# Attention and graph layer on one core: order of the parts of a step, and the softmax denominators over 32 columns with one reciprocal spread through DRAM

## The chip, the cores and the metric

The kernel runs on one core of one Trainium2 chip. The metric is the device time of one execution in microseconds (us). The kernel before takes 3855.4 us in the median of ten runs, 3853.72 to 3857.78.

## What is computed

Thirty-two samples of 512 tokens with 512 features go through two layers with the same 512 x 512 adjacency matrix. Layer 0 is attention with eight heads of 64 features under a mask, layer 1 a graph attention whose logits are a sum of two numbers per token pair. All is float32.

```python
def _L0_gnn_ref(x, adj, Wq, bq, Wk, bk, Wv, bv, Wo, bo):
    q, k, v = (x @ Wq + bq), (x @ Wk + bk), (x @ Wv + bv)     # each reshaped to (b, n, 8, 64)
    scores = jnp.einsum('bqhd,bkhd->bhqk', q, k) / jnp.sqrt(jnp.float32(HD))
    scores = scores + (1.0 - adj)[None, None, :, :] * -1000000000.0
    attn = jax.nn.softmax(scores, axis=-1)
    out = jnp.einsum('bhqk,bkhd->bqhd', attn, v).reshape(b, n, d)
    return out @ Wo + bo
def _L1_gnn_ref(x, W, a, beta, mask):
    h = jnp.einsum('bnc,cf->bnf', x, W)
    s1, s2 = h @ a[:F_, 0], h @ a[F_:, 0]
    e = leaky_relu(s1[:, :, None] + s2[:, None, :], 0.2) * mask[None, :, :]
    att = jax.nn.softmax(e, axis=2)
    return jax.nn.elu(jnp.einsum('bij,bjf->bif', att, h) + beta * h)

h = jnp.maximum(_layernorm(x), 0.0);  x = x + L0(h, adj)
h = jnp.maximum(_layernorm(x), 0.0);  x = x + L1(h, adj)
```

## The kernel before

**Products.** A 512 x 512 x 512 product is done with seven products of half size instead of eight (`seven`, line 428). Its pieces come in a fixed order: A11 with b11 into PSUM bank x, S1 with t1 into bank qz[0], S2 with t2 onto y (which ScalarE has filled with a copy of x), A12 with b21 onto x, S3 with t3 onto z = qz[1] (filled with a copy of y), S4 with b22 onto y, NA22 with t4 onto z. So the third piece waits for the copy y<-x, the fifth for the copy z<-y. The sums t1 to t4 of the right operand are made by GpSimd (POOL): `combos`, `first_combo`, `other_combos`, `fourth`. Five such products are done for each sample: v, q, k, Wo (names with _w) and the final one with W (names with _y).

**Attention.** The eight heads go in four pairs j. A *unit* (b, j) does the values of the pair before it, po<-e,v (`values`, into bank po, 16 matmul instructions of 512 columns), and then the scores of its own pair in four blocks k of 128 keys: ps<-qT,kT into the banks s, then x and y, then qz, then s again (`scores`). VectorE adds the mask to each block (e, lines 562 and 567), ScalarE takes the exponential (line 582), VectorE adds the four blocks up to es (line 579). `denominators(b, j)`, the "." in the order of a step, calls `finish` for the pair before: a product of ones with es gives pd, the denominators, each repeated on 64 partitions (line 620), VectorE takes the reciprocal in two halves of 256 columns (line 628), ScalarE copies rd onto itself to get its sum for the later check of range (line 633), and POOL multiplies the unnormalised output oT with it (line 634).

**Other parts of a step.** V, W, K, Q: the products v, Wo, k, q. D: the diagonal and the denominators of layer 1. G: gather, the four products pg<-at,hn of layer 1 (13.7 us), whose results ScalarE copies to gT. X: the three sums of POOL over gT. Y: the final product with W, followed for each quarter by the ELU: ScalarE exponential (line 811), VectorE lines 814 and 816 (and 836 ahead of them for two of the four quarters), POOL adds x1 (line 824), SP stores. N: transposes of the normalised next sample through banks po, qz and s (`turn`), with ReLU on ScalarE. H: POOL's sums over hT. U: POOL's sums over oT. r, R: loads of x for the residual, and the addition of c_row.

**Order.** TensorE, VectorE, ScalarE and POOL run their instructions in the order in which the program emits them. The parts of a step are given by a string, for most samples

```python
}.get(b, "0.VDU1.GX2.rYNRWH3.KQ")
```

in which a digit is a unit of sample b, V and Q belong to samples b and b+1, Wo to b-1, and D, G, X, Y to b-2. Work of VectorE that has slack is not emitted at once, but given to a planner (`later`, `then`, line 186) with an earliest time, a due time and a cost. It is emitted when the planner's own clocks of TensorE and VectorE (`pe(us)`, `dve(us)`) say that it fits; `need(key)` emits all that is left of a kind. The list GAP (line 44) sets due times for the sums es and for the reciprocals.

Of the kernel before, what the change touches and what calls it, by code (L numbers as in the profile page):

```python
# [9 lines left out]
F32 = mybir.dt.float32  # L10
# [3 lines left out]
AF = mybir.ActivationFunctionType  # L14
ALU = mybir.AluOpType
# [6 lines left out]
P = 128  # L22
HD = 64
# [13 lines left out]
H = 256  # L37
# [3 lines left out]

A11, A12, NA22, S1, S2, S3, S4 = range(7)

GAP = (12.0, 14.0, 28.0, 24.0)
GAPS = {0: (14.0, 1.0, 4.0, 24.0), 1: (12.0, 12.0, 2.0, 14.0)}
LAST_GAPS = (3.0, 14.0, 12.0, 3.0)

# [16 lines left out]
def kernel(  # L64
# [23 lines left out]
    nc = tc.nc  # L88
    B, N, D = x.shape
    T = N // P  # L90
    C = D // P
    NP = D // P
# [58 lines left out]
    def wtile(shape, name, tag, bufs, dt=F32):  # L151
        return work.tile(shape, dt, name=name, tag=tag, bufs=bufs)
# [12 lines left out]
    def pe(us):  # L165

        clock["pe"] += us
        till = clock["pe"] + (1.0 if at_ends[0] else 0.4)
        while True:
            due = [i for i, (_, t, _) in enumerate(ends) if t <= till]  # L170
            fits = [
                (by, i) for i, (_, t, cost, _, by) in enumerate(spare)
                if max(clock["dve"], t) + cost <= till
            ]
            if due:
                ends.pop(due[0])[2]()
            elif fits:
                run_spare(min(fits)[1])
            else:
                return  # L180
# [5 lines left out]
    def later(key, wait, by, cost, fn):  # L186

        now = max(clock["dve"], clock["pe"])
        spare.append((key, now + wait, cost, fn, now + by))

    def then(key, fn, wait=0.0):

        ends.append((key, clock["dve"] + wait, fn))
# [202 lines left out]
    def fourth(b, name, B):  # L396

        B["t4"] = wtile([P, 2, H], f"{name}4_{b}", "T", 5)
        nc.gpsimd.tensor_tensor(B["t4"], B["t2"], B["b21"], op=ALU.subtract)

    def turn(b, st):

        xs = st["x"]
        need(("x", b))
        h = [pair(b, "hT", i, "hP", 2) for i in range(2)]

        def turned(p, c):
            for t in range(T):
                nc.tensor.transpose(p[:, ts(t, P)], xs[t][:, ts(c, P)], ident)  # L409

        def second():
            for c, tag in ((2, "po"), (3, "qz")):
                p = psum.tile([P, 1 if c == 2 else 2, N], F32, name=f"pn{c}_{b}", tag=tag)[:, 0, :]
                turned(p, c)
                nc.scalar.activation(h[1][:, c - 2, :], p, AF.Relu)

        def first():
            p = psum.tile([P, 2, N], F32, name=f"pn0_{b}", tag="s")
            for c in range(2):
                turned(p[:, c, :], c)  # L420
            nc.scalar.activation(h[0], p, AF.Relu)

        for part in (second, first) if b else (first, second):
            part()
        pe(2.4)
        st["h"] = h

# [115 lines left out]
    def gap(b, j):  # L543
        return (LAST_GAPS if b == B - 1 else GAPS.get(b, GAP))[j]

# [69 lines left out]
    def finish(b, j, st):  # L615

        need("rd")
        pd = psum.tile([P, N], F32, name=f"pd_{b}_{j}", tag="pd")
        for s in range(2):
            nc.tensor.matmul(  # L620
                pd[s * HD : (s + 1) * HD, :], ones[:, :HD], st["es"][j][:, s, :], start=True, stop=True
            )
        pe(0.95)
        o = st["o"][j // 2][:, j % 2, :]
        rd = wtile([P, N], f"rd_{b}_{j}", "rd", 1)

        def divide(k):
            nc.vector.reciprocal(rd[:, ts(k, H)], pd[:, ts(k, H)])  # L628
            if k:
                then("rd", rest)  # L630

        def rest():
            nc.scalar.activation(rd, rd, AF.Copy, accum_out=rsum[:, b, j : j + 1])  # L633
            nc.gpsimd.tensor_tensor(o, o, rd, op=ALU.mult)  # L634

        finished.add((b, j))
        release()
        for k in range(2):
            later("rd", 0.0, gap(b, (j + 1) % NP) + 3.0, 1.7, lambda k=k: divide(k))

    def residual(b, st, i, tag="x1", bufs=3):

# [18 lines left out]
    def out_proj(b, st):  # L661
        x1 = st["x1"]
        st["mv"] = wtile([P, T, 2], f"mv1_{b}", "mv1", 2)
        st["s12"] = wtile([P, 2, T], f"s12_{b}", "s12", 2)
        st["hn"] = [None] * T

        def parts(k, i, p):

            n = 2 // len(x1[k])
            for u, r in enumerate(x1[k]):  # L670
                yield r[:, :, ts(i, H)], quarter(p)[:, u * n : (u + 1) * n, :]

        def add(i, k, p):
            for r, p_ in parts(k, i, p):
                nc.vector.scalar_tensor_tensor(r, p_, 1.0 / VS, r, op0=ALU.mult, op1=ALU.add)  # L675
                dve(0.75 if len(x1[k]) == 1 else 0.45)

        def one(i, k, p):
            add(i, k, p)
            if i == 1:  # L680
                norm1(b, st, (0, 1))

        def two(i, k, p, r):
            add(i, k, p)
            if i == 0:
                norm1(b, st, (2, 3))

        def more(q_):
            for i in (1, 0):
                for r, q in parts(1, i, q_):  # L690
                    nc.gpsimd.tensor_tensor(r, r, q, op=ALU.add)

        return seven(f"w{b}", wo, st["oT"], True, one, two, 1.0 / VS, more)
# [173 lines left out]
    def step(b):  # L867

        cur, nxt = states.get(b), states.get(b + 1)
        prev, old = states.get(b - 1), states.get(b - 2)

        def run(pieces):
            for _ in pieces:
                pass

        def V():
            run(proj_v(b, cur))

        def G(cs=range(C)):
            for c in cs:
                gather(b - 2, c, old)

        def y_(g):
            st = states[g]
            st["pieces"] = final(g, st)
            for _ in range(3):
                next(st["pieces"])

            B = st["gB"]
            B["t4"] = B["t2"]
            nc.gpsimd.tensor_tensor(B["t4"], B["t2"], B["b21"], op=ALU.subtract)

        def z_(g):
            run(states[g]["pieces"])

        def Y():
            y_(b - 2)
            z_(b - 2)  # L900

        def X():
            old["gB"] = combos(b - 2, "vT", old["g"])

        def G1():

            G((0, 1))
            t1 = first_combo(b - 2, "vT", old["g"][0], nc.gpsimd)
            G((2, 3))
            old["gB"] = other_combos(b - 2, "vT", old["g"], t1)  # L910

        def turned():
            turn(b + 1, nxt)
            if b + 2 < B:
                new_state(b + 2)

        def W():
            need("wa")
            fourth(b - 1, "uT", prev["oT"])
            run(out_proj(b - 1, prev))  # L920


        def H_():
            nxt["hT"] = combos(b + 1, "tT", nxt["h"])

        def K():
            fourth(b + 1, "tT", nxt["hT"])
            run(proj_k(b + 1, nxt))

        def U():  # L930
            need("rd")
            if b == B:
                prev["oT"] = other_combos(b - 1, "uT", prev["o"], prev["t1"])
            else:
                prev["oT"] = combos(b - 1, "uT", prev["o"])

        def T1():
            cur["t1"] = first_combo(b, "uT", cur["o"][0], nc.gpsimd)

        parts = {  # L940
            "V": V, "D": lambda: diagonal(b - 2, old), "G": G, "Y": Y, "N": turned, "W": W,
            "y": lambda: y_(b - 3), "z": lambda: z_(b - 3), "X": X, "g": G1,
            "K": K, "U": U, "H": H_, "r": lambda: residual(b - 1, prev, 0, *(("e", 4) if b == B else ())),
            "t": T1, "n": lambda: run_all(("hn", b - 1)), "J": judge,
            "R": lambda: residual(b - 1, prev, 1, *{B: ("e", 4), B - 1: ("x", 4)}.get(b, ())),
            "Q": lambda: run(proj_q(b + 1, nxt)),
            "c": lambda: value_row(ao, bvr), "w": row_constants,
        }
        order = {
            0: "0.V1.NH2c.3wK.Q", 1: "0.VUrR1.W2.NH3K.Q", B - 1: "0.VDU1.rRGX2.W3.t", B: "0yrR.zUWDngY",  # L950
            B + 1: "DgJY",
        }.get(b, "0.VDU1.GX2.rYNRWH3.KQ")
        unit_ = 0
        at_ends[0] = b < 2 or b >= B - 1
        for part in order:
            if part.isdigit():
                unit_ = int(part)
                unit(b, unit_)
            elif part == ".":
                denominators(b, unit_)  # L960
            else:
                parts[part]()
        states.pop(b - 3, None)
# [260 lines left out]
```

## Time and profile before

| | us |
|---|---|
| median of ten runs | 3855.4 |
| the profiled execution, its own time | 3855.6 |
| its span, first to last instruction | 3853.8 |
| TensorE busy | 3623.1 |
| VectorE busy | 2829.1 |
| ScalarE busy | 1478.0 |
| POOL busy | 1291.6 |
| TensorE's waits behind the transposes, line 409 | 160.0 |
| mean granted TensorE clock | 0.971 of full |

A group of the profile gives line, engine, operation, out<-in, shape and count, then busy time and mean ns of one, then the idle time of the engine just before it and what ended it. A line of waits gives who waited for whom, the total in us, how often, and the longest. A line of a timeline gives start and length in us, engine, line, operation, tiles, shape and count, and in brackets the idle time before it. Matmuls are pipelined: the time that one costs is the distance to the next start, not its length. The chip's DMA traffic is low, 31 GB/s in the mean.

### The profile page before, as it was taken

To read this page: it belongs to the slowest core of one execution; us is meant where nothing else is said; L and a number is where in the kernel's file an instruction comes from. 1 tells how busy PE (TensorE), PEld (TensorE's weight loads), DVE (VectorE), ACT (ScalarE), POOL (GpSimd) and SP (SyncE) were. 2 spreads that over 40 slices of the span, in tenths; PEclk is the share of its full clock that TensorE was granted. 3 is DMA by queue.
4 is the path that set the end of the run, shared out by engine and by line. 5 is a ranking of instruction groups with operands and counts; after the bars stand their busy time and mean duration, and the time that the engine had idled before them with its cause. 6 is when DMAs were issued, how large, how long until landed. Compare 5 with 4: busy or idle time off the path is not lost. (4 is left out here: it accounts for less than half of the span.)

```text
span 3853.8 us, 62639 instructions
## 1 busy us (share of the span) xinstructions
PE 3623.1 (94%) x25846; PEld 2024.3 (53%) x25846; DVE 2829.1 (73%) x4335; ACT 1478.0 (38%) x2310; POOL 1291.6 (34%) x1090
## 2 busy tenths in 40 slices
PE   9999999999999999999999999999999999999986
PEld 5555555555554555555555545555455555555543
DVE  7978767787677777677877778767777777787674
ACT  3433333343433433343434334333433333343332
POOL 5432333322333232333223332334332233322341
PEclk9999999999999999999999999999999999999998
DMA  3010111001110001111011110111110111101100
GB/s 124 17 37 4 37 36 36 34 6 34 37 36 34 20 20 37 36 34 36 4 37 36 36 34 9 31 37 36 34 35 6 36 37 36 34 4 37 31 25 26
DMA packets 88035, 120.82 MB, mean 31 GB/s; under 512 B 11904, under 2 KB 49792, under 8 KB 87744
## 3 DMA queue, kind: packets, MB, share of 16 engines
q1 hardware_dynamic: 86160, 114.91, 9.3%
q8 instruction: 205, 3.36, 0.4%
q10 hardware_dynamic: 1376, 1.57, 0.1%
q14 instruction: 86, 0.70, 0.1%
q0 software_dynamic: 208, 0.27, 0.0%
HBM read 83.11 MB, written 33.62 MB: 30 GB/s over the span
## 5 line engine op out<-in xcount | busy, mean ns | idle before, releaser
L634 POOL TENSOR_TENSOR oT<-oT,rd 128x512 f32<-128x512 f32 x128 | 170.5, 1332 | 1624.2 <-ACT rd L633 1624.2
L582 ACT ACTIVATE e<-e 128x1024 f32<-128x1024 f32 x512 | 541.1, 1057 | 191.7 <-DVE e L567 157.6
L567 DVE SCALAR_TENSOR_TENSOR e<-maskT,ps 128x1024 f32<-128x1024 uint8 x384 | 454.3, 1210 | 145.2 <-PE ps L555 145.0
L555 PE MATMUL ps<-qT,kT 64*128 64x512 f32 x2048 | 483.3, 605 | 12.4 <-DVE e L567 12.4
L605 PE MATMUL po<-e,v 128*64 128x512 f32 x2048 | 462.9, 592 | 0.0
L53 PE MATMUL pg<-at,hn 128*64 128x512 f32 x2048 | 449.1, 597 | 4.2 <-DVE dmax L788 2.1
L628 DVE RECIPROCAL rd<-pd 128x256 f32<-128x256 f32 x256 | 434.8, 1728 | 1.2 <-POOL oT L634 1.2
L579 DVE TENSOR_TENSOR es<-es,e 128x1024 f32<-128x1024 f32 x254 | 342.0, 1347 | 16.9 <-ACT e L582 1.1
L555 PEld LDWEIGHTS ps<-qT,kT 64*128 64x128 f32 x2048 | 183.9, 186 | 309.3 <-issue 214.0
L53 PEld LDWEIGHTS pg<-at,hn 128*64 128x64 f32 x2048 | 148.5, 138 | 298.3 <-issue 290.0
L605 PEld LDWEIGHTS po<-e,v 128*64 128x64 f32 x2048 | 156.6, 138 | 236.3 <-issue 226.4
L409 PE MATMUL pn<-ident,x 128*128 128x128 f32 x512 | 106.4, 378 | 160.4 <-DVE y L816 160.0
L824 POOL TENSOR_TENSOR y<-y,x 128x512 f32<-128x512 f32 x124 | 157.3, 1269 | 243.1 <-DVE y L816 202.6
L613 ACT COPY oT<-po 128x512 f32<-128x512 f32 x128 | 73.9, 577 | 397.5 <-PE po L605 397.5
L675 DVE SCALAR_TENSOR_TENSOR x<-x_w,x 128x512 f32<-128x512 f32 x32 | 22.0, 689 | 273.0 <-issue 261.5
L729 DVE CUSTOM_DVE_ANT_0 scr<-hn,wa_r 128x512 f32<-128x512 f32 x256 | 167.9, 711 | 49.0 <-ACT hn L716 49.0
L756 ACT ACTIVATE at<-at 128x512 f32<-128x512 f32 x128 | 80.4, 628 | 274.8 <-DVE at L752 274.8
L633 ACT ACTIVATE rd<-rd 128x512 f32<-128x512 f32 x128 | 80.7, 630 | 272.4 <-DVE rd L628 272.3
L334 POOL TENSOR_TENSOR rs<-rs,mhalf 128x2 f32<-128x2 f32 (+1 forms) x97 | 77.9, 804 | 318.5 <-DVE rs L333 314.8
L409 PEld LDWEIGHTS pn<-ident,x 128*128 128x128 f32 x512 | 87.5, 198 | 179.9 <-issue 179.1
L654 POOL TENSOR_TENSOR x<-x,c_row 128x512 f32<-128x512 f32 x124 | 158.5, 1300 | 49.1 <-DMA x<-in_x_dram 49.1
L814 DVE TENSOR_SCALAR y<-y 128x512 f32<-128x512 f32 x128 | 61.5, 480 | 152.0 <-ACT y L811 152.0
(221 smaller groups left out, 6794.5 us busy)
## 6 DMA issues: line engine op xcount, KB each, us to landing
x<-in_x_dram SPq DMA_DIRECT2D x128, 256.0 KB, 4.5
out_dram<-y SPq DMA_DIRECT2D x128, 256.0 KB, 2.1
x<-in_x_dram SPq DMA_DIRECT2D x63, 512.0 KB, 3.9
s<-row_s SPq DMA_DIRECT2D x32, 256.0 KB, 3.9
adj<-in_adj_dram SPq DMA_DIRECT2D x4, 256.0 KB, 7.6
wk<-in_L_gnn_Wk_dram ACTq DMA_DIRECT2D x3, 256.0 KB, 9.0
wq<-in_L_gnn_Wq_dram SPq DMA_DIRECT2D x3, 256.0 KB, 6.7
wv<-in_L_gnn_Wv_dram SPq DMA_DIRECT2D x3, 256.0 KB, 5.4
```

Of the source, the lines that this page charges most:

```text
L53: nc.tensor.matmul(out[s : s + HD], lhsT[:, s : s + HD], rhs, start=start, stop=stop, skip_group_check=onto)
L409: nc.tensor.transpose(p[:, ts(t, P)], xs[t][:, ts(c, P)], ident)
L555: nc.tensor.matmul(ps[s], st["kT"][j][rows, ts(k, P)], st["qT"][j][rows, :], start=True, stop=True)
L567: nc.vector.scalar_tensor_tensor(e, maskT[:, k, :].unsqueeze(1).to_broadcast([P, 2, N]), NEG, p, op0=ALU.mult, op1=ALU.add)
L579: (nc.gpsimd if early else nc.vector).tensor_tensor(es, one, e, op=ALU.add)
L582: nc.scalar.activation(e, e, AF.Exp)
L605: nc.tensor.matmul(po[s * HD : (s + 1) * HD, :], v[k // 2][:, k % 2, (2 * j + s) * HD : (2 * j + s + 1) * HD], e[k][:, s, :], start=k == 0 ...
L628: nc.vector.reciprocal(rd[:, ts(k, H)], pd[:, ts(k, H)])
L634: nc.gpsimd.tensor_tensor(o, o, rd, op=ALU.mult)
L654: eng.tensor_tensor(r[:, t, :], r[:, t, :], c_row, op=ALU.add)
L729: nc.vector.tensor_tensor_reduce(scr, st["hn"][t], r, 1.0, 0.0, op0=ALU.mult, op1=ALU.add, accum_out=st["s12"][:, g, t : t + 1],)
L824: (nc.vector if b == B - 2 else nc.gpsimd).tensor_tensor(yu, yu, x_[:, :, ts(i, H)], op=ALU.add)
```

## The change

**Order of a step.** For samples 2 to 30 the final product now comes directly behind its gather (g is the gather with POOL's sums among it), then a unit, then Wo and the transposes, then a unit, then k and q. M is W with the sum t4 emitted after three pieces of the product. The transposes use bank s first, then po and qz, in all samples. GAP has new values.

**Denominators.** The product of ones with es uses 32 columns of ones, four times for 256 columns of es, so that pd has (head, half of the queries) on four groups of 32 partitions and 256 columns. One reciprocal of 256 columns follows. ScalarE's copy for the sum goes to pd. One row of each group, 4 x 256 numbers, is written to DRAM by ScalarE's queue, and SP's queue reads it back twice, broadcast on 64 partitions each, into rd of 128 x 512. POOL's multiplication is as before; the planner emits it 6.0 us of its clock later.

```diff
-GAP = (12.0, 14.0, 28.0, 24.0)
+GAP = (13.0, 26.0, 14.0, 24.0)
...
-        for part in (second, first) if b else (first, second):
-            part()
+        first()
+        second()
...
-        pd = psum.tile([P, N], F32, name=f"pd_{b}_{j}", tag="pd")
+        pd = psum.tile([P, N], F32, name=f"pd_{b}_{j}", tag="pd")[:, :H]
         for s in range(2):
-            nc.tensor.matmul(
-                pd[s * HD : (s + 1) * HD, :], ones[:, :HD], st["es"][j][:, s, :], start=True, stop=True
-            )
-        pe(0.95)
+            for k in range(2):
+                r = (2 * s + k) * 32
+                nc.tensor.matmul(
+                    pd[r : r + 32, :], ones[:, :32], st["es"][j][:, s, ts(k, H)], start=True, stop=True
+                )
+        pe(0.55)
         o = st["o"][j // 2][:, j % 2, :]
         rd = wtile([P, N], f"rd_{b}_{j}", "rd", 1)
-        def divide(k):
-            nc.vector.reciprocal(rd[:, ts(k, H)], pd[:, ts(k, H)])
-            if k:
-                then("rd", rest)
-        def rest():
-            nc.scalar.activation(rd, rd, AF.Copy, accum_out=rsum[:, b, j : j + 1])
-            nc.gpsimd.tensor_tensor(o, o, rd, op=ALU.mult)
+        rq = rd[:, :H]
+        def divide():
+            nc.vector.reciprocal(rq, pd)
+            then("rd", spread)
+        def spread():
+            d = dram.tile([2, N], F32, name=f"rd_{b}_{j}", tag="rd")
+            nc.scalar.activation(pd, rq, AF.Copy, accum_out=rsum[:, b, j : j + 1])
+            nc.scalar.dma_start(d.rearrange("s (k q) -> (s k) q", k=2), rq[0:P:32, :])
+            for s in range(2):
+                nc.sync.dma_start(rd[s * HD : (s + 1) * HD, :], d[s : s + 1, :].to_broadcast([HD, N]))
+            then("rd", lambda: nc.gpsimd.tensor_tensor(o, o, rd, op=ALU.mult), 6.0)
         finished.add((b, j))
         release()
-        for k in range(2):
-            later("rd", 0.0, gap(b, (j + 1) % NP) + 3.0, 1.7, lambda k=k: divide(k))
+        later("rd", 0.0, gap(b, (j + 1) % NP) + 3.0, 1.7, divide)
...
+        def M():
+            pieces = out_proj(b - 1, prev)
+            for _ in range(3):
+                next(pieces)
+            fourth(b - 1, "uT", prev["oT"])
+            run(pieces)
...
-        }.get(b, "0.VDU1.GX2.rYNRWH3.KQ")
+        }.get(b, "0.VDU1.rgY2.RMNH3.KQ")
```

More of the change, by code (lines that the diff above doesn't have):

```diff
@@ L941, in step @@
             "V": V, "D": lambda: diagonal(b - 2, old), "G": G, "Y": Y, "N": turned, "W": W,
-            "y": lambda: y_(b - 3), "z": lambda: z_(b - 3), "X": X, "g": G1,
+            "y": lambda: y_(b - 3), "z": lambda: z_(b - 3), "X": X, "M": M, "g": G1,
             "K": K, "U": U, "H": H_, "r": lambda: residual(b - 1, prev, 0, *(("e", 4) if b == B else ())),
```

## The prediction, made before the changed kernel had run

> **What bounds the kernel now.** I read busy times first, then TensorE's waits, then the timelines of one steady step (samples 2 to 30 run one order, 29 times).
>
> ```profile
> PE 3623.1 (94%) x25846; PEld 2024.3 (53%) x25846; DVE 2829.1 (73%) x4335; ACT 1478.0 (38%) x2310; POOL 1291.6 (34%) x1090
> ...
> L628 DVE RECIPROCAL rd<-pd 128x256 f32<-128x256 f32 x256 | 434.8, 1728 | 1.2 <-POOL oT L634 1.2
> ```
>
> TensorE is busy nearly always, so work taken from VectorE counts only where TensorE waits for VectorE. TensorE's waits:
>
> ```profile
> PE pn L409 <- DVE y L816: 160.0, 29, 5.8
> PE pe L53 <- DVE as L763: 19.1, 2, 11.7
> PE ps L555 <- DVE e L567: 12.4, 33, 1.7
> ```
>
> One place, 29 times, 5.51 us each: the transposes behind the final product. The step that I use, TensorE first, then VectorE:
>
> ```profile
> 1810.32 1.90 PE L53 MATMUL qz_y<-w,vT 128*64 128x256 f32 x16
> 1812.14 0.66 PE L409 MATMUL pn<-ident,x 128*128 128x128 f32 x4
> 1818.31 2.79 PE L409 MATMUL pn<-ident,x 128*128 128x128 f32 x12 [5.50 <-DVE y L816]
> 1821.03 2.95 PE L53 MATMUL x_w<-wo,oT 128*64 128x256 f32 x16
> 1823.82 1.89 PE L53 MATMUL qz_w<-wo,oT 128*64 128x256 f32 x16
> ...
> 1834.18 3.60 PE L605 MATMUL po<-e,v 128*64 128x512 f32 x16
> 1837.71 3.70 PE L555 MATMUL ps<-qT,kT 64*128 64x512 f32 x16
> 1841.34 1.08 PE L620 MATMUL pd<-es,ones 128*64 128x512 f32 x4
> 1842.25 1.90 PE L53 MATMUL x_k<-hT,wk 128*64 128x256 f32 x16
> ```
>
> ```profile
> 1814.62 0.88 DVE L816 SCALAR_TENSOR_TENSOR y<-yq,rd,y 128x256 f32<-128x256 f32 x2
> 1816.55 0.63 DVE L814 TENSOR_SCALAR y<-y 128x512 f32<-128x512 f32 x1 [1.04 <-ACT y L811]
> 1817.29 0.88 DVE L816 SCALAR_TENSOR_TENSOR y<-qz_y,rd,y 128x256 f32<-128x256 f32 x2
> ```
>
> The last ELU of the final product reads qz until 1818.17, and the second transpose bank is qz. After the idle the clock is halved: in the stretches 1801 to 1819 and 1819 to 1835 the granted clock is 0.92 and 0.87, later 1.00. Twelve transposes take 2.72 us, against 0.109 each at full clock (sample 1, at 173.87), and the first product piece takes 2.79 against 1.73. Loss: 1.41 + 1.06 = 2.47 here. This step is 118.47 us long and the mean over 28 steps (wait ends 280.19 to 3593.20) is 118.32, so 2.3 on average.
>
> **The change, part by part** (us per steady step; SP's and POOL's new queue orders were read from the changed program).
>
> *Removed:* stall 5.51, half clock 2.3, and a 0.33 wait in unit 1 (scores for VectorE, late by two reciprocals of 3.36 at 1890.15; one of 1.73 ends in time). Sum 8.14. Without its stalls the step is about 110.
>
> *Denominators.* pd to the next product takes 0.91 now (1841.34 to 1842.25): 0.43 streaming for each of two passes, some 0.05 fill. The trace has no 32-column product. Lower end: four at once on half the columns, 0.91 - 0.43 = 0.48. Upper end: two at a time, 0.91 plus one more change of tile shape, 0.1 (the last scores' pass starts at 1840.82 and streams 0.43; pd starts at 1841.34, 0.1 late) = 1.0. The nearest row is the 16 small products of pe, 0.98 at 1886.92: 61 ns each, eight make 0.49, plus 0.1: I take 0.6. Gain 0.3 in units 1 to 3, 0.9; unit 0 below. The Trainium skill, "TensorEngine Tiling (Array Packing)", Key Properties, speaks against the edit: a change of tiling mode drains the array, while different tiles run in parallel. The trace agrees with the drain (that 0.1); by the page alone, without the 61 ns, one would write 0.43 + 0.1 and gain 0.4 a unit.
>
> *One reciprocal.* VectorE loses 1.73 four times a step. That is worth nothing further: it is off the path, except where a queue waits for it, next.
>
> *Unit 0: a new stall.* ScalarE's queue now has, of unit 0, three exponentials, the copy of rd, its DMA, the fourth exponential, then y_v<-x_v, without which v's third piece cannot start. The copy waits for the reciprocal behind the four mask additions:
>
> ```profile
> 1872.60 1.28 DVE L562 SCALAR_TENSOR_TENSOR e<-maskT,ps 128x512 f32<-128x512 uint8 x2
> 1873.80 2.34 DVE L567 SCALAR_TENSOR_TENSOR e<-maskT,ps 128x1024 f32<-128x1024 uint8 x2
> ```
> ```profile
> 1872.72 4.51 ACT L582 ACTIVATE e<-e 128x1024 f32<-128x1024 f32 x4 [0.97 <-DVE e L567]
> 1877.14 0.58 ACT L450 COPY y_v<-x_v 128x512 f32<-128x512 f32 x1
> ```
>
> Reciprocal 1876.06 to 1877.81; ScalarE starts 0.09 later (1893.51 to 1893.60 elsewhere); copy of 256 columns 0.4 (0.63 for 512); DMA issue 0.4 (0.37 to 0.52 on ACT's queue at the start; zero if it overlaps the copy); exponential 0.97; y_v copy 0.58; 0.07 to TensorE: 1880.32. The third piece of v starts at 1878.29 now: +2.03, from +1.6 to +2.4. A quicker pd gains nothing in this unit. Behind the late copy stand only q5_v and z of the same product, which are then early enough.
>
> *Final product directly behind its gather.* y's third piece needs vT2, 3.45 after the gather's end. POOL has ahead of it rd of unit 0's pair, which now waits for DRAM. From the gather's start g: sums es end at g + 5.6, reciprocal g + 7.35, ScalarE's copy behind the second gather copy g + 8.1, write 1.4 from issue (row_s<-s, 2 KB), two reads on SP 0.35 apart, 3.9 (s<-row_s, 256 KB in one; the stores of 256 KB take 2.1, x loads 4.5), so g + 14.2, a round trip of 6.1 with the waits between; POOL multiply 1.4, vT2 1.3: g + 16.9. TensorE asks at g + 13.73 + 3.45 = g + 17.2. Hidden, by the gather, with 0.3 to spare; beyond that every microsecond more of DMA costs one. POOL's power for the next sample's norm stands behind vT3, and two rows of VectorE wait for it ahead of the ELU: they end 7.1 after the product's start, the ELU is asked for at 8.0 (1807.95 now), so 0.9 to spare.
>
> ```profile
> s<-row_s SPq DMA_DIRECT2D x32, 256.0 KB, 3.9
> row_s<-s SPq DMA_DIRECT2D x32, 2.0 KB, 1.4
> ```
>
> *A unit behind the final product.* The ELU chain is unchanged: qz free 18.3 after the product's start (1799.96 to 1818.31). The unit's third scores now ask for it at 12.09 + 5.35 (po to third scores in the step shown) = 17.44: stall 0.9. VectorE adds the mask to the first scores only after the ELU, 1.2, so the fourth scores (bank s) wait 0.25 more. Sum 1.15. Next late: Wo's y copy behind the four exponentials, 0.15.
>
> *Transposes behind Wo, then a unit.* qz is free after one addition of 0.69, hidden by twelve transposes. But po, asked for next by the unit's values, is free only after ScalarE's ReLUs of the first two banks (1.02) and of po (0.6): about 2.75 after the start, against 1.9 of transposes. +0.85. The turned order (s, po, qz) puts it there.
>
> *Moved on other queues.* SP's x loads (4 x 0.4) now stand ahead of the reads of unit 2's rd; that rd holds POOL before tT4, which k needs 7 us later. The s1 row is read 1.4 + 3.9 + 0.3 behind the last dot, while VectorE has four kT rows (1.8) and three sums (3.7) and waits for hidden parts of k: some 1.4 to spare; beyond it VectorE is late for q's first bank. The out stores come behind reads that have landed before the final product's first ELU. Costed at nothing. The new GAP values only move positions in these queues, which the order read here contains.
>
> *Sum.* -8.14 - 0.9 + 2.03 + 1.15 + 0.15 + 0.85 = -4.86; times 29: -141. Edges: 12 other pd -3.6; po wait in two early steps +1.7; at the end the last rd is on the path (y_w waited 3.44 for POOL's uT), DRAM 6.2 from reciprocal to POOL against 0.84, less 1.6 of reciprocal: +3.8. Together +2. The profiled execution took 3855.6 (span 3853.8 and 1.8 around it), 0.2 above the median: 3855.6 - 139 = **3716**.
>
> **Rivals.**
> (a) *None of the new waits appears*: -8.14 - 1.2 = -9.3 a step, 3855 - 271 = 3584. For it: ScalarE is at 38%. Against it: the queue order above is fixed and in-order; all three would have to be absent, and unit 0's pd gain would count.
> (b) *The clock gate closes in the new 2 us wait of v.* Waits of 1.69 (at 79.86) left the clock at 1.00, 3.87 (at 129.50) halved it; mine lies between. Price as today, 2.3: 3716 + 67 = 3783. By the Trainium skill, "TensorE: Matmul & The Clock Gate", part 1, the clock falls after an idle window of about 3.4 us, so it would stay; the sum by the page is the 3716 above.
> (c) *DRAM round trip late by 2 to 3 us*: vT2 comes late, a round trip of 9.0 instead of 6.1 gives +2.6 x 29: 3791. For it: the 0.3 of cover, and loads at the start that took 5 to 10.
> (d) *Slower than before*: the same vT2 wait, but over 4.86 us, from a round trip of 6.1 + 0.3 + 4.9 = 11.3 on. At 12: 5.6 over, 3716 + 162 = 3878. Against it: the queues moved nothing during the gather (DMA share 0.01 from 1897 to 1911).
> (e) *The four matmuls do not run together*: 1.0 for pd, so units 1 to 3 lose 0.3 together instead of gaining 0.9: 1.2 x 29, 3751.
>
> **How the numbers follow.** Forecast 0.55 (its own range 3685 to 3745, from the ends of the DMA issue, pd at 0.48 and the po and qz waits), (a) or most of the way to it 0.10, (b) 0.11, (c) 0.12, (d) 0.06, (e) 0.04; 0.02 is left for waits that cancel the gain. The range 3650 to 3795 takes in (b), (c) and (e), and leaves out (d) and most of (a). What the measurement can tell from no change is 0.2%, 8 us. Faster 0.92, same 0.02, slower 0.06.
>
> **What would show it.** Right: no wait of pn for y, granted clock near 1.00; y_v waiting about 2 us for ScalarE 29 times; ps for VectorE about 1 us behind the final product; po for ScalarE's ReLU below 1; pd to its successor in 0.6; steps of 113.4. Wrong: a wait of y_y for POOL's vT, half clock in unit 0, or pd at 0.9.

## The result and the profile after

The changed kernel takes 3837.6 us in the median (eight runs, 3832.3 to 3843.3), against 3855.4 for the kernel before: a ratio of 0.9954 with a 95% interval of 0.9945 to 0.9962. It is faster by 17.8 us, half a per cent. The forecast was a gain of 139 us, to 3716. The profiled execution of the changed kernel took 3843.0, with a span of 3841.2 and a mean granted TensorE clock of 0.973.

First the busy times and two groups of the page of the kernel after (engine, busy us, share, instructions; then for each group its busy time and the mean of one, and the idle time ahead of it with what ended it):

```profile
PE 3586.7 (93%) x26358; PEld 1911.5 (50%) x26358; DVE 2772.6 (72%) x4207; ACT 1446.6 (38%) x2310; POOL 1390.7 (36%) x1090
...
L632 DVE RECIPROCAL rd<-pd 128x256 f32<-128x256 f32 x128 | 224.2, 1752 | 3.7 <-POOL oT L642 3.0
L623 PE MATMUL pd<-es,ones 128*32 128x256 f32 x1024 | 91.0, 430 | 128.0 <-ACT pd L638 128.0
```

The reciprocals are halved, from 434.8 us to 224.2, as the change says. The second group is the new thing: the products of the denominators stood idle for 128.0 us, all of it for ScalarE's line 638. TensorE's waits in the kernel after (who waits for whom, total us, times, longest):

```profile
PE pd L623 <- ACT pd L638: 128.0, 29, 4.4
PE ps L555 <- DVE y L823: 31.3, 29, 2.6
PE po L605 <- ACT hT L415: 22.6, 31, 0.8
...
PE y_y L53 <- POOL vT L392: 6.3, 13, 0.6
```

The wait of the transposes for the ELU (160.0 us) is gone. In its place stands one of 128.0 us, also 29 times, at the denominators of unit 0. The next two are waits that the prediction had in its sum, at about their size (1.08 and 0.78 us a step). The last, TensorE waiting for GpSimd's vT, is one that the prediction had held to be just hidden and had set down as a sign of being wrong; it comes to 0.2 us a step.

The same as a table of a steady step: the mean over 29 steps (from the product v of sample 2 to that of sample 31) of the distance from the start of each TensorE stage to the start of the next, worked out from the traces. A digit is the unit; "scores" runs from the first scores to the product of the denominators, so a wait of that product shows there.

| stage | before | after |
|---|---|---|
| transposes, Wo | 8.90 + 13.00 | 2.69 + 12.33 |
| scores 1, scores 3 | 4.24, 3.63 | 3.63, 3.63 |
| scores 2 (the unit behind the final product) | 3.63 | 5.21 |
| denominators, units 1 to 3, each | 0.91 | 0.57 |
| scores 0, denominators 0, v | 3.65 + 0.91 + 12.09 | 8.12 + 0.87 + 13.86 |
| final product | 12.19 | 12.41 |
| gather, k, q, values, diagonal | 53.37 | 53.09 |
| step | 118.33 | 117.56 |

The row of unit 0 has grown by 6.20 us; everything else together has shrunk by 6.97. TensorE at that place in the kernel before, where it does not wait:

```profile
1870.29 3.70 PE L555 MATMUL ps<-qT,kT 64*128 64x512 f32 x16
1873.92 1.08 PE L620 MATMUL pd<-es,ones 128*64 128x512 f32 x4
1874.83 1.90 PE L53 MATMUL x_v<-wv,hT 128*64 128x256 f32 x16
```

And in the kernel after, from the scores of unit 0 into v:

```profile
1863.23 3.70 PE L555 MATMUL ps<-qT,kT 64*128 64x512 f32 x16
1871.35 0.64 PE L623 MATMUL pd<-es,ones 128*32 128x256 f32 x8 [4.41 <-ACT pd L638]
1871.92 3.36 PE L53 MATMUL x_v<-wv,hT 128*64 128x256 f32 x16
1875.06 2.22 PE L53 MATMUL qz_v<-wv,hT 128*64 128x256 f32 x16
1877.11 1.90 PE L53 MATMUL y_v<-wv,tT 128*64 128x256 f32 x16
```

VectorE and ScalarE of the kernel after in the same stretch:

```profile
1866.74 2.34 DVE L567 SCALAR_TENSOR_TENSOR e<-maskT,ps 128x1024 f32<-128x1024 uint8 x2
1869.01 1.75 DVE L632 RECIPROCAL rd<-pd 128x256 f32<-128x256 f32 x1
```

```profile
1870.79 0.39 ACT L638 ACTIVATE pd<-rd 128x256 f32<-128x256 f32 x1 [1.74 <-DVE rd L632]
1870.80 0.50 ACTq L639 DMA_DIRECT2D rd<-rd  x1
1871.11 0.18 ACT L638 ACTIVATION_READ_ACCUMULATOR pd<-rd 128x1 f32 x1
1871.35 1.06 ACT L582 ACTIVATE e<-e 128x1024 f32<-128x1024 f32 x1
1875.37 0.57 ACT L450 COPY y_v<-x_v 128x512 f32<-128x512 f32 x1 [2.97 <-PE x_v L53]
```

There is one bank pd. The reciprocal of the pair before (pair 2) is emitted behind unit 0's four mask additions. It reads pd until 1870.76, and ScalarE's copy, whose destination is now pd, holds the bank until 1871.29. Only then can TensorE write the denominators of pair 3, which it asked for at 1866.93. The copy y_v, which the prediction had as the first thing to be late, waits 2.97 us for TensorE itself: by then everything is late, so TensorE never waits for it. The clock in this stretch (length in us, busy time of PE, PEld, DVE, ACT, POOL, then the granted clock, the DMA share and GB/s):

```profile
1860.00:1872.00 12.00, 7.59 (x42) 2.57 (x40) 10.98 (x14) 6.07 (x9) 0.05 (x1) 1.00 0.00 0
1872.00:1887.00 15.00, 15.00 (x130) 9.90 (x132) 5.31 (x7) 3.31 (x6) 1.27 (x1) 0.89 0.07 19
```

After the idle the half clock is back, now in v: its first two pieces start 3.14 us apart (1871.92 to 1875.06), against 1.73 for later ones (1877.11 to the next at 1878.84).

### The profile page after: what moved, and what is told of

It reads as the page before. It is cut to its first block, busy times and chain, and to the rows that moved or that the text cites. A ratio compares the mean times of both kernels' runs of the same rounds, so it can differ in the third digit from the quotient of the medians.

```text
span 3841.2 us, 64244 instructions
## 1 busy us (share of the span) xinstructions
PE 3586.7 (93%) x26358; PEld 1911.5 (50%) x26358; DVE 2772.6 (72%) x4207; ACT 1446.6 (38%) x2310; POOL 1390.7 (36%) x1090
## 5 line engine op out<-in xcount | busy, mean ns | idle before, releaser
L579 DVE TENSOR_TENSOR es<-es,e 128x1024 f32<-128x1024 f32 x254 | 415.1, 1634 | 22.4 <-ACT e L582 1.2
L498 POOL TENSOR_TENSOR qT<-qT,edge 128x256 f32<-128x256 f32 x128 | 84.9, 685 | 575.5 <-DVE qT L494 575.5
L605 PEld LDWEIGHTS po<-e,v 128*64 128x64 f32 x2048 | 143.0, 137 | 259.3 <-issue 218.2
L359 DVE TENSOR_SCALAR x<-x,mv,rs 128x512 f32<-128x512 f32 x128 | 113.7, 930 | 197.7 <-POOL rs L334 197.5
L632 DVE RECIPROCAL rd<-pd 128x256 f32<-128x256 f32 x128 | 224.2, 1752 | 3.7 <-POOL oT L642 3.0
L623 PE MATMUL pd<-es,ones 128*32 128x256 f32 x1024 | 91.0, 430 | 128.0 <-ACT pd L638 128.0
L53 PE MATMUL qz_y<-w,vT 128*64 128x256 f32 x1520 | 180.3, 379 | 2.4 <-DVE yq L843 2.4
L579 DVE TENSOR_TENSOR es<-e,e 128x1024 f32<-128x1024 f32 x127 | 168.7, 1328 | 11.4 <-PE pd L623 10.8
L53 PE MATMUL x_v<-wv,hT 128*64 128x256 f32 x1024 | 168.8, 488 | 0.0
L809 ACT COPY gT<-pg 128x512 f32<-128x512 f32 x128 | 75.0, 586 | 245.8 <-PE pg L53 244.3
## 6 DMA issues: line engine op xcount, KB each, us to landing
rd<-rd SPq DMA_DIRECT2D x256, 128.0 KB, 2.9
```

Of the source, the lines that this page charges most:

```text
L53: nc.tensor.matmul(out[s : s + HD], lhsT[:, s : s + HD], rhs, start=start, stop=stop, skip_group_check=onto)
L359: nc.vector.tensor_scalar(xs[t], xs[t], mv[:, t, 0:1], rstd[:, t : t + 1], op0=ALU.subtract, op1=ALU.mult)
L579: (nc.gpsimd if early else nc.vector).tensor_tensor(es, one, e, op=ALU.add)
L605: nc.tensor.matmul(po[s * HD : (s + 1) * HD, :], v[k // 2][:, k % 2, (2 * j + s) * HD : (2 * j + s + 1) * HD], e[k][:, s, :], start=k == 0 ...
L632: nc.vector.reciprocal(rq, pd)
```

## The experiments

All ratios are against the kernel before, run on the same chip. Stage means are as in the table above.

**Is it the place of the reciprocal?** The theory: the reciprocal of pair 2 comes too late in VectorE's queue, and the bank pd is held. Its due time in the planner is 24.0 + 3.0; with 18.0 it falls ahead of unit 0's mask additions, and nothing else in the code changes.

```diff
-        later("rd", 0.0, gap(b, (j + 1) % NP) + 3.0, 1.7, divide)
+        later("rd", 0.0, 18.0 if j == 2 else gap(b, (j + 1) % NP) + 3.0, 1.7, divide)
```

> The changed kernel with one number changed: the reciprocal of the third pair gets a due time of 18 instead of 27, which puts it among k's work on VectorE instead of behind the mask additions of unit 0. Theory P (place of that reciprocal): unit 0's 4.4 us wait of pd for ScalarE's copy goes, and with it the half clock in v; unit 0's scores, pd and v take 3.65 + 0.57 + 12.1 = 16.3 us instead of 8.12 + 0.87 + 13.86 = 22.85, so a step of 111.0 and 3837.6 - 29 x 6.5 = 3649 us. Rival D (the DRAM spread and POOL's contention with VectorE eat the gain): the wait shows up elsewhere, 3780 or more. Rival O (the order of the parts is at fault): as D, 3780 or more.

Measured: 3681.4 us (3678.8 to 3683.6), ratio 0.9548 (0.9532 to 0.9563). The step is 111.75: scores 0 are back at 3.63, the denominators at 0.57, v at 12.14. The theory holds, but 32 us less was gained than expected (3649); 27 of them are unit 1's scores, which grew from 3.63 to 4.55 a step. TensorE's waits in this run:

```profile
PE ps L555 <- DVE y L823: 30.4, 29, 2.3
...
PE ps L555 <- DVE dmax L795: 13.8, 19, 1.1
```

VectorE in a steady step of this run, from the last sum of unit 0 into unit 1:

```profile
1795.81 2.56 DVE L579 TENSOR_TENSOR es<-es,e 128x1024 f32<-128x1024 f32 x2
1798.28 1.75 DVE L632 RECIPROCAL rd<-pd 128x256 f32<-128x256 f32 x1
1800.49 0.69 DVE L532 TENSOR_TENSOR v<-qz_v,q_v 128x512 f32<-128x512 f32 x1 [0.46 <-PE qz_v L53]
...
1804.76 0.22 DVE L786 TENSOR_SCALAR bd<-pe,beta_b 128x4 f32<-128x4 f32 x1 [1.92 <-PE pe L53]
1805.02 4.67 DVE L789 SCALAR_TENSOR_TENSOR at<-ident,bd,at 128x128 f32<-128x128 f32 x4
...
1810.84 1.21 DVE L567 SCALAR_TENSOR_TENSOR e<-maskT,ps 128x1024 f32<-128x1024 uint8 x1
```

GpSimd of this run at the same time, and then the diagonal's rows in the kernel after:

```profile
1805.39 1.28 POOL L642 TENSOR_TENSOR oT<-oT,rd 128x512 f32<-128x512 f32 x1 [21.26 <-DMA rd<-rd]
1806.75 1.32 POOL L378 TENSOR_TENSOR uT<-oT,oT 128x512 f32<-128x512 f32 x1
```

```profile
1887.10 1.57 DVE L789 SCALAR_TENSOR_TENSOR at<-ident,bd,at 128x128 f32<-128x128 f32 x4
```

With room made, the planner has drawn the next pair's reciprocal (pair 3) forward, to 1798.28, ahead of v's additions. That by itself delays nothing on VectorE, which still stands idle for 1.92 us before the diagonal. But the reciprocal's way through DRAM is now over at 1805.39, and GpSimd's multiplication and the sums behind it run beside the diagonal's four rows. These take 4.67 us instead of 1.57, and unit 1's mask additions come late. The 29 steps bear this out: unit 1's scores take 5.0 us in the 18 steps in which the rows take 4.6 (GpSimd busy beside them for over 4 us), 4.0 in the 4 in which they take 3.6, and 3.63 in the other 7, in which they take 1.5 to 2.6 us.

**How much of the wait is ScalarE's copy into pd?** Here the copy goes onto its own source, so pd is free when the reciprocal has read it.

```diff
-            nc.scalar.activation(pd, rq, AF.Copy, accum_out=rsum[:, b, j : j + 1])
+            nc.scalar.activation(rq, rq, AF.Copy, accum_out=rsum[:, b, j : j + 1])
```

> The changed kernel with ScalarE's copy of rd onto rd instead of onto the bank pd, so that pd is free at the reciprocal's end and not at the copy's. Theory P: the wait of pd in unit 0 only gets shorter by the copy's 0.55 us (1870.79 to 1871.35), its releaser becomes VectorE's reciprocal, the clock still falls: 3837.6 - 29 x 0.55 = 3822, plus up to 10 for the later DMA. Rival B (the copy into the bank is at fault): the wait goes, 3650.

Measured: 3824.0 us (3823.3 to 3825.6), ratio 0.9917 (0.9900 to 0.9933). TensorE's first wait in this run:

```profile
PE pd L623 <- DVE rd L632: 112.3, 29, 3.9
```

The copy is the last 0.5 us of the wait, 13.6 us of the whole (3837.6 less 3824.0); the other 3.9 are the place of the reciprocal. After 3.9 us of idle v still takes 13.56.

**Each half of the change alone.** First the new order of the step and the new GAP with the old denominators (64 columns, two reciprocals, no DRAM). The edits are shown in part, against the changed kernel:

```diff
-            for k in range(2):
-                r = (2 * s + k) * 32
-                nc.tensor.matmul(
-                    pd[r : r + 32, :], ones[:, :32], st["es"][j][:, s, ts(k, H)], start=True, stop=True
-                )
+            nc.tensor.matmul(
+                pd[s * HD : (s + 1) * HD, :], ones[:, :HD], st["es"][j][:, s, :], start=True, stop=True
+            )
...
-        later("rd", 0.0, gap(b, (j + 1) % NP) + 3.0, 1.7, divide)
+        for k in range(2):
+            later("rd", 0.0, gap(b, (j + 1) % NP) + 3.0, 1.7, lambda k=k: divide(k))
```

> The new order, transposes and due times with the denominators as before (two products of 64 columns and 512, two reciprocals, no DRAM). Here the planner puts the third pair's reciprocals among q's work. Theory P: no wait in unit 0; step = 110.07 without stalls, + 1.6 (scores behind the final product) + 0.85 (po behind the transposes) + 0.6 (two reciprocals ahead of unit 1's mask) + 0.2 = 113.3, so 3837.6 - 29 x 4.2 = 3715. Rival D: about the same, 3715. Rival O: 3800 or more.

Then the old order, the old GAP and the old transposes with the new denominators:

```diff
-GAP = (13.0, 26.0, 14.0, 24.0)
+GAP = (12.0, 14.0, 28.0, 24.0)
...
-        first()
-        second()
+        for part in (second, first) if b else (first, second):
+            part()
...
-        }.get(b, "0.VDU1.rgY2.RMNH3.KQ")
+        }.get(b, "0.VDU1.GX2.rYNRWH3.KQ")
```

> The order, transposes and due times of before with the new denominators (four products of 32 columns, one reciprocal, DRAM). Here the planner puts the third pair's reciprocal among q's work. Theory P: the old 5.5 us stall and its half clock stay; gain 4 x 0.34 for pd and 0.6 in unit 1, 2.0 a step, less 4 at the end: 3855 - 57 + 4 = 3802. Rival D: 3837 or slower.

Measured: the order alone 3698.4 us (3696.1 to 3700.7), ratio 0.9592 (0.9576 to 0.9608), step 112.80, half a microsecond less than expected. The denominators alone 3798.0 us (3796.1 to 3801.3), ratio 0.9849 (0.9832 to 0.9865), step 116.05. Their two gains are 5.53 and 2.28 us a step, 7.81 together; the change that has both gains 0.77. So 7.0 us a step are lost in the meeting of the two. In both of these runs the reciprocals of pair 2 lie among q's work, ahead of unit 0, and the wait of pd in the steady steps is absent. In the second the wait of the transposes for the ELU is back, first in TensorE's waits:

```profile
PE pn L409 <- DVE y L823: 161.0, 29, 6.4
```

**The place alone, without 32 columns and without DRAM.** A rival was that the stall needs the new denominators: the small products, the copy into the bank or the DMA. So the old denominators, in the new order, got an earliest time of 33 for pair 2, which puts both reciprocals of 256 columns behind unit 0's mask additions. The edit is against the run of the new order alone:

```diff
         for k in range(2):
-            later("rd", 0.0, gap(b, (j + 1) % NP) + 3.0, 1.7, lambda k=k: divide(k))
+            later("rd", 33.0 if j == 2 and b > 1 else 0.0, gap(b, (j + 1) % NP) + 3.0, 1.7, lambda k=k: divide(k))
```

> As e3 (new order, denominators of before, no DRAM and no 32 columns), with the third pair's two reciprocals held back until they stand behind unit 0's mask additions. Theory P (the place alone makes the stall): pd of unit 0 waits for the second reciprocal, 9.31 + 3.36 us after the unit's start against 7.2, 5.5 us, and the clock halves as after every such wait, 2.3: 3698 + 29 x 7.8 = 3924. Rival: the stall needs ScalarE's copy or the DRAM spread, then within 30 us of 3698.

Measured: 3927.0 us (two runs, 3926.5 and 3927.4), ratio 1.0186 (1.0165 to 1.0206). TensorE's first wait in this run:

```profile
PE pd L620 <- DVE rd L628: 168.6, 31, 5.7
```

A kernel with none of the new denominators has the stall, and with two reciprocals it is 1.3 us longer than in the change: one more reciprocal of 1.73, less the copy's hold of the bank of 0.5. Against the run of the new order alone, which differs in this one line, it is 229 us slower. The rival falls.

**Mending the second wait too.** The due time as in the first experiment, and an earliest time of 8.0 for pair 3, so that its reciprocal isn't drawn ahead of v's additions.

```diff
-        later("rd", 0.0, gap(b, (j + 1) % NP) + 3.0, 1.7, divide)
+        later("rd", 8.0 if j == 3 else 0.0, 18.0 if j == 2 else gap(b, (j + 1) % NP) + 3.0, 1.7, divide)
```

> As e1, and the reciprocal of the fourth pair may be emitted 8 us of the planner's clock later, which puts it back behind the diagonal, where the changed kernel has it. In e1 it stood ahead of v's additions, and unit 1's scores waited 0.9 us a step for the diagonal's VectorE rows. Theory P with the later waits as forecast: 3681 - 29 x 0.92 = 3654, scores of unit 1 at 3.63. If that wait has another source, 3681 stays.

Measured: 3658.1 us (3654.9 to 3658.2), ratio 0.9486 (0.9470 to 0.9501). The diagonal's four rows take 1.55 to 1.86 us in all 29 steps, unit 1's scores are at 3.63 again, and the step is 111.1. Its remaining waits:

```profile
PE ps L555 <- DVE y L823: 29.1, 29, 2.0
PE po L605 <- ACT hT L415: 22.6, 31, 0.8
...
PE y_y L53 <- POOL vT L392: 7.5, 12, 0.9
```

The first two are in the prediction's sum; the third is the wait for vT that it had held to be hidden. Nothing else of size is left in a steady step.

**The turned order of the transposes.** The prediction put 0.85 us a step to the new order s, po, qz. On top of the last kernel, the order po, s, qz, so that ScalarE's ReLU of po comes first and is done when the values ask for the bank:

```diff
-        def second():
-            for c, tag in ((2, "po"), (3, "qz")):
+        def second(chunks):
+            for c, tag in chunks:
...
-        first()
-        second()
+        second(((2, "po"),))
+        first()
+        second(((3, "qz"),))
```

> As e5, with the transposes through po first, then s, then qz. Forecast of the prediction: po is late by ScalarE's ReLU of bank s ahead of po's, 0.85 a step (measured 0.73 wait). With po's ReLU first the wait goes: e5 less 29 x 0.8 = about 3631. Rival: qz or s is then late instead, within 5 us of e5.

Measured: 3633.1 us (3628.1 to 3636.0), ratio 0.9421 (0.9405 to 0.9436). The wait of po is gone, the transposes take 1.90 instead of 2.69: 0.79 of the 0.85.

**The wait of the scores behind the final product.** Two quarters of the final product need a sum before their ELU. On top of the last kernel, one of them, in bank y, keeps it in that bank instead of in one of the three buffers of the tag y, which the out stores hold too.

```diff
-            s = wtile([P, N], f"yq_{b}_{i}_{k}", "y", 3)
+            s = p if i == 0 else wtile([P, N], f"yq_{b}_{i}_{k}", "y", 3)
```

> As e6, with the sum yq of the quarter (0,1) of the final product written onto its own bank y instead of into one of the three y buffers, so that the exponential of this quarter needs no buffer that a store still reads. In the changed kernel that exponential starts at 1922.87, released by the store of the first quarter, 0.95 after its sum is ready (1921.92), and the last quarter's waits in turn for the buffer of yq. Theory: the rest of the wait behind the final product (unit 2's scores 5.20 against 3.63 us) is this chain; without it qz is free 0.6 us before it is asked for, scores 3.7, 3633 - 29 x 1.5 = 3590. Rival: the chain is bound by VectorE's own rows, then the wait shrinks by 0.3 at most, 3624.

Measured: 3614.7 us (3606.8 to 3622.3), ratio 0.9381 (0.9365 to 0.9398); the step of the profiled execution is 109.6. Unit 2's scores fall from 5.20 to 3.70, as the theory had it (its rival: 0.3 at most), but Wo grows from 12.40 to 13.40 and gives two thirds of it back, so that the time misses the 3590 expected. TensorE's waits in this run:

```profile
PE qz_w L53 <- DVE x L683: 20.4, 21, 2.0
...
PE qz_w L53 <- POOL uT L399: 6.7, 6, 1.2
```

Once TensorE reaches Wo earlier, Wo's pieces meet VectorE's addition of line 683 and GpSimd's uT, which had been done in time before. Which of their own causes makes these late was not tried. This is the fastest version of the study, 240.7 us below the kernel before by the medians.

A second buffer for pd, by which TensorE's next product would not have to wait for the reciprocal, was not tried. In the changed kernel pd fills only 256 of the 512 columns of its tile.

## Why the prediction was right and wrong

**The step that failed: "Unit 0: a new stall", +2.03.** Its mechanism was half right. The chain was read correctly: reciprocal behind four mask additions, ScalarE's copy behind the reciprocal. The first to wait for that copy, though, was taken to be v's third piece, through the exponential and the copy y_v, and so the sum counted only what came late there. But another waits for the copy's end before that, TensorE's next product of the denominators, because the copy writes into the one bank pd. That product comes right behind the scores, 4.4 us before v's third piece. The term was to hold 2.03; the row of unit 0 grew by 6.20: 4.47 more up to the product of the denominators (the wait is 4.41 in the step shown), 2.07 of half clock in v (13.86 for 12.09) and the denominators (0.87 for 0.57), less 0.34 of the shorter product. The excess of 4.17 is the whole error of the step: forecast 113.4, measured 117.56; 29 times, it is 121 us, as much as the forecast of 3716 was off. It was within reach of the prediction's own numbers. The reciprocal that it worked out ends at 1877.81, its copy 0.09 + 0.4 later at 1878.3, and v begins at 1874.83, so the product of pair 3, 0.91 ahead of it, is asked for at 1873.92: 4.4 us. "A quicker pd gains nothing in this unit" was written in that very paragraph, without the question when pd becomes free. The trace of the kernel before even has one such wait, in an early step, which the prediction used only for the clock (the 3.87 of rival (b)):

```profile
129.50 1.43 PE L620 MATMUL pd<-es,ones 128*64 128x512 f32 x4 [3.87 <-DVE rd L628]
```

**The rest of the sum held.** Without the term of unit 0 the forecast is 118.33 - 6.89 = 111.4 a step; the run with both reciprocals placed, where that stall is gone, has 111.1. That the two lie so close is in part luck, since single terms are off by up to 0.4 either way:

- *Removed*, 8.14, given back 0.85 and 0.15 at the transposes and Wo: net -7.14. Transposes, Wo and unit 1's scores together went from 26.14 to 18.65, -7.49; 0.28 of the difference is unit 1, whose scores had stood 0.61 above 3.63 where the prediction counted the wait of 0.33. The wait of po was 0.73, and the run with po first put 0.79 to it.
- *Denominators*, 0.91 to 0.6, was 0.57 in units 1 to 3. The estimate from the drain that the Trainium skill states ("TensorEngine Tiling (Array Packing)", Key Properties) and the bare streaming time, 0.1 and 0.43 by the trace of the kernel before, was 0.53; the measured value lies between the two.
- *The unit behind the final product*, 1.15, was 1.58. "The ELU chain is unchanged" was not quite so: in some steps its third exponential waits for a store of out that still holds the buffer. ScalarE of the kernel after, in one such step:

```profile
1918.84 0.91 ACT L818 ACTIVATE y<-yq,rd 128x256 f32<-128x256 f32 x2 [2.08 <-DVE yq L843]
1922.87 0.91 ACT L818 ACTIVATE y<-yq,rd 128x256 f32<-128x256 f32 x2 [3.12 <-DMA out_dram<-y]
```

  The sum that this exponential reads was ready at 1921.92, 0.95 earlier. TensorE's wait there was 1.62 us, against 0.76 in a step without it.
- *vT2 through DRAM*, hidden with 0.3 to spare: it was missed by 0.2 on average (6.3 us in 13 of 29 steps). In the step around 1900 the way through DRAM was not at fault: from ScalarE's copy (1904.41) to GpSimd's multiplication (1909.66) it took 5.25 us, where 6.1 had been put. The reciprocal ahead of it was late. It ended 9.95 us after the gather's start instead of 7.35, since the sums es before it ran beside GpSimd's sums and took 6.6 us, against 3.8 alone; the last section has rows of both.
- *Edges*, +2, were +10: the two profiled executions differ by 12.6 us (3855.6 and 3843.0), 29 steps by 22.3. Sample 2 begins 5.1 us later than before, mostly by the first Wo (18.15 instead of 12.20), which waits for GpSimd's oT, not foreseen; from the last of the steady steps to the end it is 4.7 us longer, among it 3.25 of y_w's wait for uT (3.44 to 6.69), which had been put at 3.8.

**The rivals.** (a) *No new wait* did not occur: of the three waits in the sum those of the scores and of po are in the trace, and in the place of v's stands the longer one of pd. (b) *The clock gate closes in v* did occur, though not in a wait of 2 us but after one of 4.4; its price, 1.8 in v and 0.3 in the denominators, was near the 2.3 given. As to waits of about 2 us, on which the prediction gave it little chance, the runs are divided; the last section has the rows. (c) *DRAM late* and (d), its slower form, did not occur: the reads of rd landed in 2.9 us in the median where 3.9 had been put. (e) *The four products one after the other* falls with the 0.57. The outcome, a gain nearly cancelled by a wait, stood in the prediction only as the 0.02 left over.

**What is shown and what is not.** That the place of pair 2's reciprocal makes the stall is shown from both sides: moved ahead, the stall goes; moved behind in the old denominators, it appears. That the change's two halves conflict through it is shown by the runs of each half alone. That GpSimd's work makes the diagonal's rows long, in the run with the earlier reciprocal, rests on the two going together in its 29 steps and on both being gone in the run with both reciprocals placed. Why the planner puts the reciprocal ahead of unit 0 with either half and behind it with both was not taken apart: the GAP values, the shorter costs and the order differ together.

## What to carry to other kernels

When a change moves an instruction in a queue, ask of every buffer that it reads or writes when that buffer comes free, and who asks for it first; here the first to wait was the next writer of a single buffer, not the next reader of the result. A destination for a value that nobody needs is not free either: here it lengthened the hold of the only bank by 0.5 us, 29 times. After one wait is mended, look at what a planner draws forward into the room, and at what then runs beside it on another engine; and measure the halves of a change by themselves: here 5.53 and 2.28 us a step made 0.77 together.

## What the runs showed of the hardware that had not been expected

- Idle of about 2 us halves the clock in some places and not in others. In the kernel after, a wait of 2.06 us was followed by scores at full clock; in the run with the earlier reciprocal one of 1.93 was followed by half clock. The eight scores' instructions take 2.16 us in the one and 3.11 in the other. TensorE of the first, then of the second:

```profile
1105.68 2.16 PE L555 MATMUL ps<-qT,kT 64*128 64x512 f32 x8 [2.06 <-DVE y L823]
```

```profile
2399.18 1.99 PE L555 MATMUL ps<-qT,kT 64*128 64x512 f32 x8
2403.10 3.11 PE L555 MATMUL ps<-qT,kT 64*128 64x512 f32 x8 [1.93 <-DVE y L823]
2406.14 1.08 PE L623 MATMUL pd<-es,ones 128*32 128x256 f32 x8
```

  The granted clock was 0.69 from 2403 to 2406 in the second, and 1.00 from 1105 to 1130 in the first. In the run with the copy in place a wait of 2.64 left it at 1.00; a wait of 2.08 in the run with po first brought 0.62. So the length alone doesn't decide between 1.9 and 2.6 us. The waits of up to 3.9, 4.4 and 5.7 us that recur in the steady steps of three runs raised v's mean from 12.1 to between 13.1 and 13.9. The Trainium skill ("TensorE: Matmul & The Clock Gate", part 1) gives an idle window of about 3.4 us that runs freely; the long waits agree with it, the half clock behind 1.93 us does not, and the measurement decides.
- A DMA issued on ScalarE's queue (0.50 us) began 0.01 us after the copy ahead of it and ran beside it; the next exponential started 0.56 after the copy's start, where the prediction had put 0.4 + 0.4.
- VectorE's sums es took 2.16 us each beside GpSimd's sums, and those 2.14, against 1.27 for each alone. VectorE of the kernel after, two such sums with GpSimd idle and two beside its sums, and then GpSimd at the second place:

```profile
1873.45 2.55 DVE L579 TENSOR_TENSOR es<-es,e 128x1024 f32<-128x1024 f32 x2
...
1898.32 4.33 DVE L579 TENSOR_TENSOR es<-es,e 128x1024 f32<-128x1024 f32 x2
```

```profile
1895.86 1.28 POOL L642 TENSOR_TENSOR oT<-oT,rd 128x512 f32<-128x512 f32 x1 [18.43 <-DMA rd<-rd]
1897.22 2.14 POOL L378 TENSOR_TENSOR uT<-oT,oT 128x512 f32<-128x512 f32 x1
1899.43 2.14 POOL L379 TENSOR_TENSOR oT<-oT 128x512 f32<-128x512 f32 x1
```

  The mean of these sums rose from 1347 to 1634 ns, that of x<-x,mv at line 359 from 730 to 930. Two waits of TensorE stand at the end of such rows: unit 1's in the run with the earlier reciprocal (the diagonal's rows, 4.67 us for 1.57), and the one for vT in the step around 1900. In the run with both reciprocals placed, where GpSimd's work comes later, the diagonal's rows are back at 1.55; no run shows the second wait without it.
- With 155 MB moved instead of 121, the median load of x took 7.0 us instead of 4.5, and the store of out 2.5 instead of 2.1. The second is what the ELU meets above.
